# Gated cross attention: where the next quad's attention scores stand among TensorE's products

## The chip, the cores and the metric

The kernel runs on one core of one Trainium2 chip. The metric is device time in microseconds for one execution, the median over several runs. The profile comes from one profiled execution on that core; its span is the time from the first to the last instruction.

## The reference

For each of 8 batches, x has 1024 rows of 1024 numbers and the memory has 64 rows of 512. Everything is float32.

```python
memory_proj = einsum('bme,de->bmd', memory, W_mem)
scores = einsum('bnd,bmd->bnm', hidden_states, memory_proj) / sqrt(D)
attn = softmax(scores, axis=-1)
memory_context = einsum('bnm,bmd->bnd', attn, memory_proj)
gate_input = concatenate([hidden_states, memory_context], axis=-1)
gate = sigmoid(einsum('bnf,df->bnd', gate_input, W_gate) + b_gate)
fused = hidden_states + gate * memory_context
out = rmsnorm(fused, norm_w)
```

Here hidden_states is x, and rmsnorm divides a row by the root of its mean square and multiplies by norm_w (all ones).

## The kernel before, in words

**Quads.** The rows of x are taken in 16 quads of 512 rows, two to a batch (QPB is 2). For each quad the large product is x times the upper half of W_gate, 512 by 1024 times 1024 by 1024. The lower half of W_gate is folded into the memory beforehand (mgd), so that the context's part of the gate needs only the 64 attention weights of a row.

**Products.** The large product is done by a scheme of Strassen's kind with seven products in place of eight, at two levels. The outer level has seven outer products, in the order 1, 6, 7, 5, 4, 2, 3 (ORDER). Each is made of seven inner products named A, B, C, D, A again, E and F. One inner product is two matmuls of 128 by 128 by 256. So a quad has 49 inner products, and the kernel counts them as slots: SLOTS is 49, and slot 0 is the first inner product of outer product 1. Outer product number i in the order has the slots 7i to 7i + 6.

**Operands.** The left operands are quarters of the quad, transposed: A[q, r, h], in tiles a11, a12, a21 and a22, written by transpose_x on VectorE (eight transposes a quad). From them outer_s makes S1 to S4 on VectorE; S3 overwrites a21. For each outer product, inner_s makes four more sums on GpSimd, in tiles l2 (two buffers, two parts of two sums). Results are gathered in the gate tiles O by sums on VectorE (fin) and GpSimd (pre); every inner product has one of five PSUM banks, which come free when VectorE or ScalarE has read them.

**Attention.** scores(q) makes the scores of a quad, transposed: 16 matmuls of 128 rows by 64 columns of weights, in which two matmuls at a time go to the two column halves of the array (tile psT). ScalarE copies them to sT, TensorE transposes them back (sc), softmax_a and softmax_b run on VectorE and ScalarE, and TensorE transposes the weights (pa). In the outer products 5, 4, 2 and 3 a context block stands between the second A and E: 16 matmuls of 64 rows by 128 columns, two at a time on the two row halves, half of which make the context (pc) and half of which add the context's part of the gate to the banks A, F, E and D.

**After the products.** sigmoid on ScalarE, times the context on VectorE (gated), plus the rows of x by an accumulating DMA that GpSimd issues (residual), the mean square on ScalarE (square), and norm on VectorE, in two halves a row block, with the store behind the second.

**What sets the order.** The order on each engine is the order of the program text (pin keeps it). plan(q) writes down what else happens at which slot: at(slot, f) runs f before the inner product of that slot, and mid((q, o), f) runs f right behind the context block of outer product o, before VectorE's first two sums of that block. An engine runs its instructions in that order and waits for each one's inputs and buffers.

The names that matter below:

- scores (lines 295 to 309): 16 matmuls and ScalarE's copy.
- outer_s (254 to 266): S3 and S4 among others.
- transpose_x (239 to 252).
- add_bias (371 and 372): an accumulating DMA on GpSimd's queue, once a batch; load_mg (366 to 369) loads what it adds to.
- norm (603 to 622), placed by the list named when (799 to 809) at the end of outer products 4 and 3. Outer product 4 ends at slot 35, so its offsets count from there.
- plan (530 to 563) and product (676 to 683).

Of the kernel before, what the change touches and what calls it, by code (L numbers as in the profile page):

```python
# [20 lines left out]
def tile_gated_cross_attention_rmsnorm(  # L21
# [46 lines left out]
    QPB = N // QT  # L68
# [31 lines left out]
    def t4k(pool, shape, tag, name):  # L100
        return pool.tile(shape, F32, tag=tag, name=name)
# [33 lines left out]
    for k in range(KD):  # L135
        t = t4k(*((gpool, [P, D], "gate") if k < 7 else (apool, [P, D], "s4")), f"w2_{k}")
# [383 lines left out]
    def at(slot, fn, *args):  # L520
        due.setdefault(slot, []).append(lambda: fn(*args))

    def mid(key, fn, *args):
        beside.setdefault(key, []).append(lambda: fn(*args))
# [5 lines left out]
    def plan(q):  # L530
        t0 = SLOTS * q
        nxt = q + 1 < NQ
        order = [o for o, _ in ORDER]
        for i, o in enumerate(order):
            for part, t in ((0, 1), (1, 5)):
                if i + 1 < len(order):
                    at(t0 + 7 * i + t, inner_s, q, order[i + 1], part)
                elif nxt:
                    at(t0 + 7 * i + t, inner_s, q + 1, order[0], part)
        at(t0 + 7, scores, q)  # L540
        at(t0 + 7, outer_s, q, 3)
        at(t0 + 7, outer_s, q, 4)
        at(t0 + 9, transpose_scores, q)
        at(t0 + 10, softmax_a, q)
        at(t0 + 13, softmax_b, q)
        at(t0 + 18, transpose_attn, q)
        at(t0 + 21, attn_difference, q)
        if not nxt:
            at(t0 + 5, load_last)
            return  # L550
        at(t0 + 2, load_xq, q + 1)
        for t in (2, 3):
            mid((q, 5), transpose_x, q + 1, t, 0)
            mid((q, 2), transpose_x, q + 1, t, 1)
        for i, t, half in ((36, 0, 0), (38, 1, 0), (43, 0, 1), (45, 1, 1)):
            at(t0 + i, transpose_x, q + 1, t, half)
        mid((q, 3), outer_s, q + 1, 1)
        mid((q, 3), outer_s, q + 1, 2)
        if (q + 1) % QPB == 0:
            at(t0 + 10, load_mp, (q + 1) // QPB)  # L560
            at(t0 + 49, load_mg, (q + 1) // QPB)
        if q % QPB == 0:
            at(t0 + 8, add_bias, q // QPB)

    for o in (2, 3):
        w1_place(o)
# [97 lines left out]
    def sqrt_table():  # L664

        t = t4k(small, [P, 1], "warm", "warm")
        pin(nc.scalar.activation(t, eps_sb, AF.Sqrt))

    def outer_product(q, o, ext):
# [113 lines left out]
        if o in (4, 3) and q + 1 == NQ:  # L783
            c, d = 2 * ext[0], 2 * ext[0] + 1
            if o == 3:
                sqrt_table()
            first = (4, 5) if o == 4 else (3, 3)
            at(slot + first[0], last_root, d)
            at(slot + first[1], last_root, c)
            for i, t in enumerate((d, c)):  # L790
                for h_ in range(2):
                    at(slot + first[1] + 1 + 2 * i + h_, last_norm, t, h_)
        elif o in (4, 3):

            row = ext[0]
            c, d = 2 * row, 2 * row + 1
            for t in (d, c):
                at(slot + 5, residual, q, t)
            if row == 0:
                when = (17, 18, 23, 29, None, None)  # L800
            else:
                when = (17, 18, 23, 25, 26, 28)
            at(slot + when[0], square, q, c)
            at(slot + when[1], square, q, d)
            for w_, (t, h_) in zip(when[2:], ((c, 0), (c, 1), (d, 0), (d, 1))):
                if w_ is None:
                    mid((q + 1, 4), norm, q, t, h_)
                else:
                    at(slot + w_, norm, q, t, h_)
# [3 lines left out]
    for q in range(NQ):  # L813
        plan(q)
        for o, ext in ORDER:
            outer_product(q, o, ext)
# [29 lines left out]
```

## Time and profile before

| what | value |
|---|---|
| median of 3 runs | 980.77 us (980.74 to 981.12) |
| span of the profiled execution | 979.4 us |
| granted TensorE clock | 0.996 of full |
| TensorE (PE) busy | 964.8 us, 99% |
| VectorE (DVE) busy | 820.4 us, 84% |
| GpSimd (POOL) busy | 730.5 us, 75% |
| ScalarE (ACT) busy | 324.9 us, 33% |
| scores of one quad to scores of the next | 55.05 us |

The profile is a page with the busy time of each engine, the chain of work that ended last, and groups of instructions. A trace behind it answers for stretches of the span: what ran when, who waited for whom, and the chain in order of time. PE is the matmuls, PEld the loading of weights into the array, which can run beside a matmul. A float32 matmul leaves two records in the trace, so an inner product of two matmuls shows as x4 and the scores of a quad as x32. Ends of matmul records are modelled; starts are the firmer number. Busy time of an engine that nobody waits for costs nothing.

### The profile page before, as it was taken

How to read it: one execution, taken by the hardware profiler on the slowest of the kernel's cores; microseconds unless marked ns; L12 is line 12 of the kernel's file. 1: busy time of each engine (PE TensorE's matmuls, PEld its weight loads, DVE VectorE, ACT ScalarE, POOL GpSimd, SP SyncE). 2: the span in 40 equal slices, each digit the busy share in tenths (PEclk: the TensorE clock that was granted, in tenths of full speed). 3: DMA queues.
4: the chain of work that ended last, by engine and by line, in shares of the span. 5: the costliest groups of instructions: out<-in, count | busy, mean ns of one | idle time of the engine just before them, and what ended most of it. 6: DMA issues, size and time to landing. Idle time of an engine off the chain costs nothing.

```text
span 979.4 us, 14277 instructions
## 1 busy us (share of the span) xinstructions
PE 964.8 (99%) x4938; PEld 769.8 (79%) x4938; DVE 820.4 (84%) x1487; ACT 324.9 (33%) x602; POOL 730.5 (75%) x881
## 2 busy tenths in 40 slices
PE   9999999999999999999999999999999999999995
PEld 6546888888887888888887888888887888888873
DVE  3888788979797988979797988979797988979787
ACT  1100234151433334151433334151433334151434
POOL 3366877878787877878787877878787877878772
PEclk9999999999999999999999999999999999999998
DMA  9865264482918374482918374482818364482612
GB/s 372 258 153 145 39 120 107 103 188 62 186 65 165 108 141 106 102 190 65 183 65 164 111 138 105 107 184 66 182 65 168 110 136 104 108 184 68 169 65 86
DMA packets 71255, 128.32 MB, mean 131 GB/s; under 512 B 12432, under 2 KB 49296, under 8 KB 70928
## 3 DMA queue, kind: packets, MB, share of 16 engines
q1 hardware_dynamic: 61760, 93.34, 35.3%
q0 software_dynamic: 9280, 33.56, 18.5%
q8 instruction: 39, 0.64, 0.3%
q10 hardware_dynamic: 144, 0.52, 0.2%
q14 instruction: 32, 0.26, 0.1%
HBM read 87.56 MB, written 39.85 MB: 130 GB/s over the span
## 4 chain that ended last, share of the span: by engine, by line
PE 96%; DVE 2%; DMA 1%; issue 0%; ACT 0%; POOL 0%; DVEq 0%; ACTq 0%
PE kA L92 20%; PE pc L92 12%; PE kE L92 11%; PE kF L92 10%; PE kD L92 10%; PE kC L92 10%; PE kB L92 10%; PE psT L92 6%; PE pg L92 5%; PE pm L92 3%; DVE gate L95 1%; DMA memq<-in_mem 1%; DVE gate L660 0%; PE pa L342 0%; PE sc L316 0%
## 5 line engine op out<-in xcount | busy, mean ns | idle before, releaser
L95 POOL TENSOR_TENSOR gate<-gate,u 128x256 f32<-128x256 f32 x336 | 270.4, 835 | 115.7 <-DVE u L95 110.1
L582 ACT ACTIVATE gate<-gate 128x512 f32<-128x512 f32 x128 | 79.0, 629 | 400.1 <-DVE gate L95 400.1
L95 POOL TENSOR_TENSOR l<-a 128x256 f32<-128x256 f32 x128 | 128.9, 1007 | 60.4 <-DVE a L95 55.8
L248 DVE STREAM_TRANSPOSE a<-xq 128x512 f32<-128x512 f32 x128 | 137.9, 1098 | 4.0 <-DMA xq<-in_x 4.0
L92 PE MATMUL pc<-mg,attnT 64*128 64x256 f32 x512 | 127.4, 389 | 0.0
L611 DVE SCALAR_TENSOR_TENSOR gate<-gate,ss,nw_sb 128x512 f32<-128x512 f32 x120 | 126.0, 1060 | 1.1
L92 PE MATMUL kD<-it,l 128*128 128x256 f32 x448 | 115.0, 379 | 0.0
L92 PE MATMUL kB<-it,l 128*128 128x256 f32 x448 | 115.0, 379 | 0.0
L92 PEld LDWEIGHTS pc<-mg,attnT 64*128 64x128 f32 x512 | 90.6, 186 | 29.7 <-issue 21.2
L92 PE MATMUL kA<-w,a 128*128 128x256 f32 x384 | 98.7, 379 | 0.4 <-ACT u L726 0.4
L92 PEld LDWEIGHTS kD<-it,l 128*128 128x128 f32 x448 | 85.1, 190 | 11.6
L92 PEld LDWEIGHTS kB<-it,l 128*128 128x128 f32 x448 | 85.1, 190 | 11.6
L95 DVE TENSOR_TENSOR gate<-gate,pc 128x512 f32<-128x512 f32 x128 | 87.0, 680 | 5.8 <-ACT gate L582 5.8
L95 POOL TENSOR_TENSOR l<-s 128x256 f32<-128x256 f32 x96 | 75.7, 789 | 10.8 <-PE kF L92 10.7
L92 PEld LDWEIGHTS kA<-w,a 128*128 128x128 f32 x384 | 71.6, 190 | 10.2 <-ACT u L726 0.8
L726 ACT COPY u<-kA 128x256 f32<-128x256 f32 x112 | 40.5, 362 | 102.1 <-PE kA L92 99.9
L92 PE MATMUL kE<-it,a 128*128 128x256 f32 x256 | 69.0, 392 | 0.0
L95 DVE TENSOR_TENSOR u<-u,kB 128x256 f32<-128x256 f32 x112 | 45.5, 406 | 28.1 <-PE kB L92 24.9
L92 PE MATMUL kA<-t,s 128*128 128x256 f32 x256 | 67.4, 386 | 0.0
L92 PE MATMUL kC<-w,l 128*128 128x256 f32 x256 | 65.7, 379 | 0.0
L92 PE MATMUL kF<-w,l 128*128 128x256 f32 x256 | 65.7, 379 | 0.0
L596 ACT ACTIVATE junk<-gate 128x1024 f32<-128x1024 f32 x60 | 63.5, 1059 | 2.1 <-DMA gate<-in_x 1.2
(123 smaller groups left out, 1996.6 us busy)
## 6 DMA issues: line engine op xcount, KB each, us to landing
xq<-in_x SPq DMA_DIRECT2D x64, 512.0 KB, 9.6
gate<-in_x POOLq DMA_DIRECT2D x60, 512.0 KB, 7.8
out<-gate SPq DMA_DIRECT2D x60, 512.0 KB, 2.6
w<-in_w_gate_t SPq DMA_DIRECT2D x8, 512.0 KB, 11.0
w<-in_w_gate_t SPq DMA_DIRECT2D x2, 2048.0 KB, 15.6
mg<-mgd SPq DMA_DIRECT2D x16, 256.0 KB, 4.0
mpd<-mpT SPq DMA_DIRECT2D x4, 512.0 KB, 3.8
mgd<-mpq SPq DMA_DIRECT2D x16, 128.0 KB, 2.6
```

Of the source, the lines that this page charges most:

```text
L92: pin(nc.tensor.matmul(o, lhsT, rhs, start=start, stop=stop, skip_group_check=True))
L95: pin(eng.tensor_tensor(o, a, b, op))
L248: nc.vector.transpose(A[key][:, :, r * P : (r + 1) * P], chunks(xq[q][:, 4 * t : 4 * t + 4, :], KD)[:, half * KH : (half + 1) * KH],)
L582: pin(nc.scalar.activation(g, g, AF.Sigmoid))
L596: nc.scalar.activation(junk, O[q, t], AF.Square, accum_out=ss[:, t % 2 : t % 2 + 1])
L611: nc.vector.scalar_tensor_tensor(g[:, cols], g[:, cols], rstd[:, t % 2 : t % 2 + 1], nw_sb[:, cols], ALU.mult, ALU.mult,)
L726: pin(nc.scalar.copy(p1, kb["A"]))
```

## The change

The change moves instructions in time and alters none of them: every engine has as many as before. It is meant to bring two kinds of small matmul next to each other on TensorE.

- The scores of quad q + 1 are computed in quad q, right behind the context block of outer product 3 and before its E. Only quad 0 keeps its scores at slot 7.
- S3 moves from slot 7 to slot 6 and S4 from slot 7 to slot 20 (quads 1 to 15), since neither has to stand behind the scores any longer.
- The last two transposes of the next quad move from slots 43 and 45 to slots 42 and 43, so that the scores find them done.
- The norm halves of the fourth row block, which stood at slots 12 and 14 of the next quad (35 + 26 and 35 + 28, less 49), move to slots 15 and 18.
- The bias is added at slot 4 in place of slot 8, except in quad 0.

```diff
-        at(t0 + 7, scores, q)
-        at(t0 + 7, outer_s, q, 3)
-        at(t0 + 7, outer_s, q, 4)
+        if q == 0:
+            at(t0 + 7, scores, q)
+        at(t0 + (6 if q else 7), outer_s, q, 3)
+        at(t0 + (20 if q else 7), outer_s, q, 4)
         at(t0 + 9, transpose_scores, q)
...
-        for i, t, half in ((36, 0, 0), (38, 1, 0), (43, 0, 1), (45, 1, 1)):
+        for i, t, half in ((36, 0, 0), (38, 1, 0), (42, 0, 1), (43, 1, 1)):
             at(t0 + i, transpose_x, q + 1, t, half)
+        mid((q, 3), scores, q + 1)
         mid((q, 3), outer_s, q + 1, 1)
         mid((q, 3), outer_s, q + 1, 2)
...
         if q % QPB == 0:
-            at(t0 + 8, add_bias, q // QPB)
+            at(t0 + (4 if q else 8), add_bias, q // QPB)
...
             if row == 0:
                 when = (17, 18, 23, 29, None, None)
             else:
-                when = (17, 18, 23, 25, 26, 28)
+                when = (17, 18, 23, 25, 29, 32)
```

## The prediction

> **What bounds the kernel now.** I read the page first, then what TensorE waited for, then one steady stretch of the span, then the chain of waits in that stretch, the weight loads and the VectorE timeline.
>
> The page: busy time, and the chain that ended last by engine.
>
> ```profile
> PE 964.8 (99%) x4938; PEld 769.8 (79%) x4938; DVE 820.4 (84%) x1487; ACT 324.9 (33%) x602; POOL 730.5 (75%) x881
> ...
> PE 96%; DVE 2%; DMA 1%; issue 0%; ACT 0%; POOL 0%; DVEq 0%; ACTq 0%
> ```
>
> The waits of TensorE in the whole span (total us, times, longest), its costliest row, and then one quad, from its scores (psT) to the scores of the next: length, busy time of each engine with counts, clock, DMA.
>
> ```profile
> PE kA L92 <- ACT u L726: 1.6, 3, 1.1
> ```
>
> ```profile
> 531.16:586.21 55.05, 55.05 (x299) 45.23 (x300) 47.31 (x88) 19.83 (x36) 44.13 (x54) 1.00 0.62 135
> ```
>
> TensorE is never idle inside a quad, its clock is full, and no engine holds it up: DVE works 47.31 of 55.05 us, GpSimd 44.13. So only fewer or cheaper TensorE microseconds can shorten the quad. That all matmuls stay the same does not settle it, because the chain shows that equal matmuls do not cost the same (start, us, what):
>
> ```profile
> 530.30 0.86 PE kF L92 x4
> 531.16 3.60 PE psT L92 x32
> 534.77 1.06 PE kA L92 x4
> 535.83 0.86 PE kB L92 x4
> ...
> 575.45 0.86 PE kA L92 x4
> 576.31 0.41 PE pc L92
> ...
> 578.24 1.06 PE kE L92 x4
> 579.30 0.86 PE kF L92 x4
> ```
>
> A product (four records of 128 rows by 128 columns) takes 0.86 us, 0.216 a record. The first product after the scores takes 1.06, and so does the first after the context block (pc): 0.20 us more. The scores themselves are 32 records, two at a time on the two column halves, so 16 x 0.216 = 3.45; they take 3.60, 0.15 more. The context block is 16 records on the two row halves, 8 x 0.216 = 1.73, and takes 578.24 - 576.31 = 1.93, 0.20 more. The weight loads say where this goes:
>
> ```profile
> 199.64 0.84 PEld L92 LDWEIGHTS kF<-w,l 128*128 128x128 f32 x4
> 200.81 3.22 PEld L92 LDWEIGHTS psT<-a,mpb 128*64 128x64 f32 x32 [0.33 <-issue]
> ```
>
> In kF the loads run one record ahead of their matmul (the first load at 199.64, its matmul at 199.86 in the TensorE timeline). At the first score the load starts only at 200.81, with its matmul, after 0.33 us in which the loads stood still and waited for nothing that the profile shows.
>
> So one quad has ten changes of array shape: into and out of four context blocks, into and out of the scores. The price list is 0.20 us into a context block, 0.20 back to full products, 0.15 into the scores. Check: 49 products x 0.864 = 42.34; four context blocks x 1.73 = 6.91; scores 3.45; the transposes of scores and weights 2 x 0.22 = 0.44; changes 5 x 0.20 + 4 x 0.20 + 0.15 = 1.95. Sum 55.09, measured 55.05.
>
> [...] 0.15 to 0.20 us at every change, none inside a block where only the tile changes. [...] here 64 columns take 137 ns and 128 take 190, which fits the entry into the scores being 0.05 cheaper. [...]
>
> **The change, part by part.**
>
> Scores of quads 1 to 15 go from in front of outer product 6 to behind the context block of outer product 3 of the quad before, still in front of that product's E. Before, per quad: full to rows, rows to full (product 3), full to columns, columns to full (scores): 0.20 + 0.20 + 0.15 + 0.20 = 0.75. After: full to rows 0.20, rows to columns, columns to full 0.20. Rows to columns is nowhere in the trace. Bounds: nothing (the load could run ahead), or two full changes, 0.35, as if the array went through its whole shape. I take 0.15, the measured entry into the scores, since what is waited for (end of the last matmul, then one load of 64 columns that nothing hides) is the same from either side. Then 0.55 after, 0.20 us saved a quad, 15 quads: 3.0 us. Quad 0 keeps its scores at slot 7, and quad 15 has no next, so its tail is as before.
>
> New waits of the moved scores. They read all four transposed tiles of the next quad. The last two transposes go from slots 43 and 45 to 42 and 43. The VectorE timeline there:
>
> ```profile
> 572.11 0.42 DVE L95 TENSOR_TENSOR gate<-gate,kF 128x256 f32<-128x256 f32 x1 [0.44 <-PE kF L92]
> ...
> 574.07 0.38 DVE L95 TENSOR_TENSOR u<-u,kB 128x256 f32<-128x256 f32 x1
> ...
> 576.33 0.39 DVE L95 TENSOR_TENSOR u<-u,kD 128x256 f32<-128x256 f32 x1
> ```
>
> At 572.11 VectorE is ahead of TensorE, so no backlog comes in. Behind that sum stand, after the change, transpose (1.11), gate product (0.69), transpose (1.11): with the overlap of neighbours seen in this timeline about 2.6 us, so both are done near 575.2. The scores would start at 578.2 and touch these tiles half way, 1.73 us later: 4.7 us to spare. Queued behind the two transposes is the sum with kB, 1.1 us later, done near 575.5. For it waits the bank that the context block reuses as kF, written from 576.78 on in the TensorE timeline: 1.2 us to spare. The sum with kD ends as before, near 576.7, since the same work stands in front of it; its bank is written again at 577.64. On ScalarE the copy of the scores now waits in front of two sigmoids that need product E, which comes behind the scores anyway: nothing.
>
> S3 at slot 6 and S4 at slot 20, 1.23 and 1.22 us on VectorE. Before, S3 waits for the scores (1.47 idle) and VectorE is idle 1.35 more at 536.80. After, S3 falls between two sums of product 1, with those idle times as cover; GpSimd's halves for product 7 start when S3 is there, about at the start of product 6 as before (it stood idle 3.7 us for it). S4 costs 1.2 us near slot 20, where VectorE had small idle times (0.23, 0.26, 0.26) and is next waiting for TensorE at 549.33. Two norm halves (1.06 each, slots 12 and 14 to 15 and 18) leave the crowded stretch in front of it. From 536.80 to 549.33 there are 12.5 us; the work there was 11.5 and becomes 12.7, of which 0.2 can spill; each bank concerned has over 1.5 us. Hidden by TensorE's products: nothing.
>
> GpSimd's bias DMA (0.83 us of issue, three times in all) from slot 8 to 4: its data's load waits only for the last context block, now some 5 us ahead of slot 0, so it does not hold the queue behind it (two residual DMAs, two halves for product 6). Nothing.
>
> What GpSimd loses is the 3.6 us of scores between the halves for product 6 and their use at slot 8. These were done at 530.7 for a use at 535.8; after, counted from the start of product 1, two of them start as TensorE leaves product 3 and the four with the two DMA issues need about 5.2 us (rows of 0.7 to 1.05 and 0.89), against 6.9 us to slot 8. Close, but free.
>
> Sum: 15 x 0.20 = 3.0 us off 980.77: 977.8.
>
> **The rivals.**
>
> Rows to columns is free. For it: inside a shape loads run ahead. Against: every change seen in this trace stops the loads 0.33 us. Then 0.35 a quad, 15 x 0.35 = 5.2 us: 975.6.
>
> Rows to columns costs both full changes, 0.35. Nothing in the trace speaks for it but that it has no such change. Then no gain: 980.8, the same.
>
> Slower: a bank or a GpSimd half comes late every quad, where the scores at slot 7 had let both engines catch up (DVE idle 2.8, GpSimd 3.7 there). The tightest margins above are 0.9 to 1.7 us. If one of them is overrun so that TensorE stands 0.5 us a quad, the change is 15 x (0.5 - 0.2) = 4.5 us: 985.3. Against it: at 572.11 and 563.07 VectorE waits for TensorE, so backlogs do not carry over, and the moved scores give the same 3.6 us of slack at slot 47.
>
> **How the numbers follow.** My forecast has 0.74, free change 0.10, full price 0.09, stall 0.07. Forecast and free change are faster by over 0.2% (2.0 us): faster 0.84; same 0.09; slower 0.07. The range takes the free change in (975.6, so 975.4), and above the forecast it goes to 979.0, where 1.2 of the 3.0 us are lost to stalls in a few quads; what is left out is no gain and slower, 0.16.
>
> **What would show it.** In the chain of the changed kernel: context block 1.93, psT 3.60 directly behind it, then kE 1.06, and in front of product 6 a kA of 0.86; scores to scores 54.85 us in place of 55.05; no wait of TensorE in a steady quad. psT of 3.45 would show the free change; psT of 3.8 the full price. A wait of PE for DVE, POOL or ACT repeated in each quad, most likely at kB or kC of product 6 or at kF or kD in the context block of product 3, would prove the forecast wrong.

## The result and the profile after

| | before | after |
|---|---|---|
| median of 6 runs each, us | 980.94 (980.74 to 981.18) | 990.66 (989.37 to 991.94) |
| ratio | 1 | 1.0099 (95%: 1.0086 to 1.0112) |
| span of the profiled execution, us | 979.4 | 987.5 |

The change costs 9.7 us where a gain of 3.0 was forecast. The page of the changed kernel, busy time and the chain by engine:

```profile
PE 965.9 (98%) x4938; PEld 770.4 (78%) x4938; DVE 821.4 (83%) x1487; ACT 326.9 (33%) x602; POOL 737.2 (75%) x881
...
PE 80%; DMA 9%; DVE 3%; ACT 3%; POOL 2%; issue 2%; DVEq 0%; POOLq 0%; ACTq 0%
```

TensorE's busy time is up by 1.1 us only, and no engine is busy for a larger share of the span than before. What is new is in the chain: 9% of it are now DMA, 1% before. Most of what the span grew by is idle time behind transfers. First, though, the part that was forecast, in the chain of waits of the changed kernel around the moved scores (start, us, what):

```profile
246.67 0.41 PE pc L92
...
248.59 3.60 PE psT L92 x32
252.20 1.06 PE kE L92 x4
253.26 0.86 PE kF L92 x4
```

The context block takes 248.59 - 246.67 = 1.92, the scores directly behind it 3.60, the product behind them 1.06: the three numbers of the forecast. So going from row halves to column halves costs the 0.15 us that was taken for it, and 0.20 us a quad are saved. The stretches of two quads (quads are counted from 0), scores to scores, with busy time by engine, show that something else eats them (length, then PE, PEld, DVE, ACT, POOL, clock, DMA):

```profile
192.20:248.52 56.32, 55.25 (x298) 45.23 (x296) 47.14 (x89) 19.93 (x36) 44.53 (x55) 1.00 0.58 127
248.52:303.57 55.05, 55.05 (x299) 45.30 (x297) 47.70 (x89) 19.84 (x36) 43.85 (x54) 1.00 0.56 120
```

Forecast was 54.85. The odd quads (second of a batch) take 55.03 to 55.05, the first of them 54.94. The even quads (first of a batch, 2 to 14) take 56.33, 55.96, 56.02, 56.75, 57.39, 55.40 and 56.22, at the full clock and with TensorE idle. Over 54.85 the even quads have 10.1 us, the odd ones 1.2; 11.3 less the 3.0 saved is 8.3, and the span grew by 8.1. Which waits these are, the list of waits says (us in total, times, longest; L598 is the square, with junk as its output, and L728 the copy u):

```profile
ACT junk L598 <- DMA gate<-in_x: 24.7, 7, 4.7
...
PE kA L92 <- ACT u L728: 8.6, 9, 1.9
```

```profile
PEld kC L92 <- POOL l L95: 4.8, 15, 0.7
```

Before, kA waited 1.6 us for u, three times, at the end of the span (from 944 us on). The other 7.0 us are new: in six of the seven even quads (all but quad 12) the second A of outer product 5 waits for u, ScalarE's copy that frees its bank. The chain through one of them (start, us, what):

```profile
199.90 1.05 POOL gate L588
200.95 14.01 DMA gate<-in_x
...
216.16 1.15 ACT junk L598 x2
...
217.33 1.28 ACT L603
...
220.47 0.38 ACT u L728
...
220.90 1.13 PE kA L92 x4
```

Read from below: TensorE's kA at 220.90 starts when u is done at 220.85. That copy stood in ScalarE's queue behind two squares, a table load and the copies of the attention weights, and the first square waited for a residual DMA that GpSimd issued at 200.95 and that landed 14.01 us later. The same stretch of ScalarE's timeline in both kernels, after and then before:

```profile
211.00 0.37 ACT L728 COPY u<-kA 128x256 f32<-128x256 f32 x1 [2.47 <-PE kA L92]
214.98 1.06 ACT L598 ACTIVATE junk<-gate 128x1024 f32<-128x1024 f32 x1 [3.61 <-DMA gate<-in_x]
...
220.47 0.37 ACT L728 COPY u<-kA 128x256 f32<-128x256 f32 x1
```

```profile
211.85 0.37 ACT L726 COPY u<-kA 128x256 f32<-128x256 f32 x1 [2.47 <-PE kA L92]
212.12 1.06 ACT L596 ACTIVATE junk<-gate 128x1024 f32<-128x1024 f32 x1
...
218.17 0.37 ACT L726 COPY u<-kA 128x256 f32<-128x256 f32 x1 [0.58 <-PE kA L92]
```

The issue of that transfer and the second A of product 5 in the kernel before, in the timelines of GpSimd and TensorE, and then the same A in the changed kernel:

```profile
198.09 0.88 POOL L586 DMA_DIRECT2D gate<-in_x  x1 [0.19 <-issue]
```

```profile
220.50 1.03 PE L92 MATMUL kA<-t,s 128*128 128x256 f32 x4
```

```profile
220.90 1.13 PE L92 MATMUL kA<-t,s 128*128 128x256 f32 x4 [1.07 <-ACT u L728]
```

Before, ScalarE came to the square at 212.12, just as the transfer landed (issued 198.09, landed 212.04), and later was 0.58 us early at u. That copy was done at 218.54 for an A that started at 220.50, so 1.96 + 0.58 = 2.54 us of delay could be absorbed. After, ScalarE is free at 211.37 and waits 3.61 us; 3.61 - 2.54 = 1.07, which is what kA waits. The transfer takes as long as before, 14.0 us; it is the distance from its issue to the square that shrank, from 14.0 to 10.4 us, which is the length of the scores. They used to stand between the two and now stand in front of the issue. That the two transfers take the same time is the sum of two effects, as the first experiment shows.

The second new wait is smaller: kC waits for GpSimd. In the odd quads, and in quad 12, it is kC of product 5. Timelines of TensorE, VectorE and GpSimd of the changed kernel in quad 3:

```profile
273.39 1.03 PE L92 MATMUL kB<-it,l 128*128 128x256 f32 x4
274.35 1.13 PE L92 MATMUL kC<-t,l 128*128 128x256 f32 x4
275.32 1.03 PE L92 MATMUL kD<-it,l 128*128 128x256 f32 x4
```

```profile
272.31 1.40 DVE L95 TENSOR_TENSOR s<-a,s 128x1024 f32<-128x1024 f32 x1
```

```profile
272.59 1.71 POOL L95 TENSOR_TENSOR l<-s 128x256 f32<-128x256 f32 x1
```

The starts of B, C and D are 0.96 and 0.97 us apart in place of 0.86, so 0.2 us are lost a quad. GpSimd's sum for C took 1.71 us, where the same sum for product 5 takes 0.72 and 0.73 in the last two kernels below, without S4 beside it; here it ran beside S4, which the change put here. In the other even quads it is kC of product 4, behind the stall: VectorE's sum waits for the late copy u, and GpSimd's sums for product 4 stand behind sums that need VectorE's (in quad 2 GpSimd waits 1.86 us for it).

### The profile page after: what moved, and what is told of

Same layout as the page of the kernel before. It is cut to its first block, busy times and chain, and to the rows that moved or that the text cites. A ratio compares the mean times of both kernels' runs of the same rounds, so it can differ in the third digit from the quotient of the medians.

```text
span 987.5 us, 14301 instructions
## 1 busy us (share of the span) xinstructions
PE 965.9 (98%) x4938; PEld 770.4 (78%) x4938; DVE 821.4 (83%) x1487; ACT 326.9 (33%) x602; POOL 737.2 (75%) x881
## 4 chain that ended last, share of the span: by engine, by line
PE 80%; DMA 9%; DVE 3%; ACT 3%; POOL 2%; issue 2%; DVEq 0%; POOLq 0%; ACTq 0%
PE kA L92 15%; PE pc L92 12%; PE kE L92 9%; DMA gate<-in_x 9%; PE kF L92 8%; PE kC L92 8%; PE kD L92 7%; PE kB L92 7%; PE psT L92 6%; PE pg L92 5%; PE pm L92 3%; DVE gate L95 1%; POOL l L95 1%; ACT junk L598 1%; ACT L603 1%
## 5 line engine op out<-in xcount | busy, mean ns | idle before, releaser
L95 POOL TENSOR_TENSOR gate<-gate,u 128x256 f32<-128x256 f32 x336 | 291.9, 897 | 120.5 <-DVE u L95 118.6
L613 DVE SCALAR_TENSOR_TENSOR gate<-gate,ss,nw_sb 128x512 f32<-128x512 f32 x120 | 123.0, 1035 | 1.1
L95 POOL TENSOR_TENSOR l<-a 128x256 f32<-128x256 f32 x128 | 103.1, 805 | 25.1 <-PE kA L92 19.3
L95 POOL TENSOR_TENSOR l<-s 128x256 f32<-128x256 f32 x96 | 88.2, 919 | 40.2 <-PE kF L92 40.2
L95 DVE TENSOR_TENSOR gate<-gate,kE 128x256 f32<-128x256 f32 x112 | 45.5, 419 | 42.9 <-PE kE L92 41.1
L92 PEld LDWEIGHTS kA<-w,a 128*128 128x128 f32 x384 | 71.8, 190 | 10.1 <-ACT u L728 0.8
L728 ACT COPY u<-kA 128x256 f32<-128x256 f32 x112 | 40.5, 361 | 109.7 <-PE kA L92 107.5
L598 ACT ACTIVATE junk<-gate 128x1024 f32<-128x1024 f32 x60 | 63.5, 1058 | 25.6 <-DMA gate<-in_x 24.7
## 6 DMA issues: line engine op xcount, KB each, us to landing
xq<-in_x SPq DMA_DIRECT2D x64, 512.0 KB, 10.1
```

The costliest lines, as they stand in the source:

```text
L92: pin(nc.tensor.matmul(o, lhsT, rhs, start=start, stop=stop, skip_group_check=True))
L95: pin(eng.tensor_tensor(o, a, b, op))
L598: nc.scalar.activation(junk, O[q, t], AF.Square, accum_out=ss[:, t % 2 : t % 2 + 1])
L613: nc.vector.scalar_tensor_tensor(g[:, cols], g[:, cols], rstd[:, t % 2 : t % 2 + 1], nw_sb[:, cols], ALU.mult, ALU.mult,)
L728: pin(nc.scalar.copy(p1, kb["A"]))
```

## The experiments

The theory after this: two losses, one from the residual DMAs through ScalarE's queue, in even quads, and one from S4 at slot 20. A first rival to it: the moved scores themselves are at fault, since GpSimd and VectorE lost their 3.6 us to catch up. Edits are against the changed kernel unless said otherwise; the kernel before, run on the same chips, took 980.8 to 980.9 us.

**The bias back at slot 8.** In the changed kernel the bias DMA stands in front of the two residual DMAs in GpSimd's queue.

```diff
-            at(t0 + (4 if q else 8), add_bias, q // QPB)
+            at(t0 + 8, add_bias, q // QPB)
```

> The changed kernel with the bias DMA back at slot 8 (behind the two residual DMAs in GpSimd's software queue), everything else as changed. Theory A (the bias DMA stands in front of the residual DMAs in the same queue in the first quad of each batch, the squares on ScalarE wait for the residuals, ScalarE copies the first half of product 5 late, TensorE's second A of product 5 waits): the waits of kA for ScalarE in the even quads go (about 7 stalls, 8.6 us with their dearer first records), ScalarE's wait for the residuals falls from 24.7 us to under 6, and the time falls to about 981.5. What stays is 0.2 us a quad at kC of product 5. Rival B (the 3.6 us that the scores took between residual and squares are missing, whatever the bias does): the stalls stay at half or more, time 985 or over. Rival C (S4 at slot 20 is the cause): no change, 989 to 991.

Measured 984.52 us (983.79 to 985.94), ratio 1.0038 (1.0025 to 1.0051): 6.1 us better than the change. From the list of waits of this kernel, the row of the residuals:

```profile
ACT junk L598 <- DMA gate<-in_x: 14.0, 7, 2.5
```

The second residual of quad 2 now lands 12.00 us after its issue in place of 14.01; over the seven even quads the means are 12.4 and 13.8. ScalarE's wait falls from 24.7 to 14.0 us, and the new waits for u are all but gone (kA 1.7, as before). So the bias in front makes the second residual 1.4 us later on average, 2.0 in quad 2. In the kernel before, with the bias behind it too, the mean was 13.7: with the scores moved the transfer itself is 1.3 us quicker, for a reason that was not taken apart, and the bias in front takes that back. The expectation had under 6 us of ScalarE's wait and about 981.5. The 14.0 us that stay are 2.0 us a batch, which fit into the 2.54 us of room and hardly stop TensorE. What is left of TensorE's loss is kC of product 5 or 4, and one quad of 57.50 us in which a norm half took 3.90 us; more of that below.

**S4 back at slot 7, and both together.**

```diff
-        at(t0 + (20 if q else 7), outer_s, q, 4)
+        at(t0 + 7, outer_s, q, 4)
```

> The changed kernel with S4 back at slot 7, the bias still at slot 4. Theory A with its second part (S4 on VectorE at slot 20 runs beside GpSimd's sum for kC of product 5 and makes it 1.7 us long in place of 0.7, so that kC waits 0.2 us in nearly every quad): kC of product 5 starts on time, 13 to 14 fewer waits, 2.6 us; the stalls at A of product 5 in the even quads stay. Time about 987. Rival C (S4 is behind the stalls too): about 978 to 981. Rival D (S4 at slot 7 without the scores' 3.6 us in front of it delays VectorE): kB or kC of product 6 wait, time not below 989.

> The changed kernel with both back: bias at slot 8, S4 at slot 7. Theory A in both parts: only the saving of the moved scores is left, 0.2 us in 15 quads, period 54.85 us, time about 978.0, faster than before by 0.3%. If it is not below 980.5, a third cause (missing slack of the scores, rival B, or the moved norm halves) is at work.

S4 alone: 986.01 us, ratio 1.0050 (1.0035 to 1.0065). The wait at kC of product 5 is gone. The stalls for u stay, but at half the size (4.2 us in place of 8.6), so that most of what this run gains comes from them: its residuals land sooner (13.58 us after the issue in place of 15.07 in quad 10), and why was not taken apart. Both: 980.30 us, ratio 0.9995 (0.9987 to 1.0004), with no new stall at u and none at that kC: the two edits account for both losses. But of the saving of 3.0 only 0.5 comes out, where 978 was expected: S4 at slot 7 has its own price. In the timelines of TensorE and VectorE of the kernel with both:

```profile
320.22 1.03 PE L92 MATMUL kA<-w,a 128*128 128x256 f32 x4
321.13 1.13 PE L92 MATMUL kB<-it,l 128*128 128x256 f32 x4
322.10 1.03 PE L92 MATMUL kC<-w,l 128*128 128x256 f32 x4
```

```profile
315.10 1.71 DVE L95 TENSOR_TENSOR s<-a,s 128x1024 f32<-128x1024 f32 x1
...
320.67 0.41 DVE L95 TENSOR_TENSOR gate<-gate,kD 128x256 f32<-128x256 f32 x1
```

Here kB of product 7 needs the bank of kD of product 6, which VectorE reads only at 320.67. Starts are 0.91 and 0.97 apart: 0.16 us lost, and quads take 55.00 to 55.01. S4 took 1.71 us here (1.22 in the kernel before), with GpSimd's sums beside it.

**The scores alone.** The kernel before, with only the scores moved.

```diff
-        at(t0 + 7, scores, q)
+        if q == 0:
+            at(t0 + 7, scores, q)
...
+        mid((q, 3), scores, q + 1)
```

> The kernel before with only the scores of quads 1 to 15 moved behind the context block of product 3: S3 and S4 at slot 7, transposes at 43 and 45, norm halves at 12 and 14, bias at 8. Theory A: the same saving as with bias and S4 put back, about 978, if VectorE catches up by slot 21 with 2.4 us of S3 and S4 at slot 7 and no pause in front; up to 980 if some sums come late. Rival B (the scores' own time was the slack that the residual needed): stalls at A of product 5 also here, 985 or over.

Measured 1023.09 us, ratio 1.0433 (1.0415 to 1.0450): the expectation missed by over 40 us. Even quads take 60.3 to 60.5 us, odd ones 55.6. The VectorE, GpSimd and TensorE timelines of one even quad:

```profile
207.94 0.75 DVE L613 SCALAR_TENSOR_TENSOR gate<-gate,ss,nw_sb 128x512 f32<-128x512 f32 x1
...
210.07 4.68 DVE L613 SCALAR_TENSOR_TENSOR gate<-gate,ss,nw_sb 128x512 f32<-128x512 f32 x1
```

```profile
209.23 0.82 POOL L372 DMA_DIRECT2D mg<-in_b_gate  x1
```

```profile
210.87 1.03 PE L92 MATMUL kA<-w,a 128*128 128x256 f32 x4
215.46 2.08 PE L92 MATMUL kB<-it,l 128*128 128x256 f32 x4 [3.56 <-DVE gate L95]
217.33 1.72 PE L92 MATMUL kC<-w,l 128*128 128x256 f32 x4
218.89 1.03 PE L92 MATMUL kD<-it,l 128*128 128x256 f32 x4
```

A norm half that takes 0.75 us at 207.94 takes 4.68 when it starts 0.84 us behind the issue of the bias DMA. The sums behind it come late, kB of product 7 stands for 3.56 us, and then kB and kC take 3.43 us together (215.46 to 218.89) in place of 1.73. That is 3.56 + 1.70 = 5.3 us a batch, seven times, 37 of the 45 us over the forecast. The starts of quad 3, against those of a quad of 54.85, give the 0.8 us of the odd ones: 0.28 at kB of product 7, 0.12 in front of the transposes of the weights and 0.37 at kC of product 5. No wait for u is new (kA 1.7). So the rival is right in part: the moved scores alone do not bring the stall at u, but without them VectorE and GpSimd come late elsewhere, and the other edits of the change do real work. The bias at slot 4 keeps it away from that norm half.

**S4 at slot 5, with the bias at 8 and at 6.** At slot 5 S4 runs ahead of the crowded stretch of slots 6 to 9.

```diff
-        at(t0 + (20 if q else 7), outer_s, q, 4)
+        at(t0 + (5 if q else 7), outer_s, q, 4)
...
-            at(t0 + (4 if q else 8), add_bias, q // QPB)
+            at(t0 + 8, add_bias, q // QPB)
```

> The changed kernel with the bias DMA at slot 8 and S4 at slot 5, where VectorE stood idle for 1 us in front of product E of outer product 1 and GpSimd's sums there have 2 us to spare; S3 stays at 6. Theory A (bias in front of the residuals, S4 beside GpSimd's sum for kC of product 5, and S4 at 7 too late for the bank of kB of product 7): all three losses gone, period 54.85 us, time about 978.0, 0.3% under before. If kB of product 7 still waits as with S4 at slot 7, S4's place was not its cause and the time is 980. If S4 right behind the residual DMAs is drawn out by GpSimd's work for them, kB of product 6 waits and the time is over 981.

Measured 1016.22 us, ratio 1.0362 (1.0339 to 1.0385), again far off. The odd quads take 54.85, the forecast, so slot 5 costs TensorE nothing, though S4 takes 2.4 us there beside two of GpSimd's sums, in place of 1.22. In seven even quads the norm half is held again:

```profile
208.70 4.68 DVE L613 SCALAR_TENSOR_TENSOR gate<-gate,ss,nw_sb 128x512 f32<-128x512 f32 x1
```

It starts 0.84 us behind the issue (207.86), as in the run above. The next run has the bias at `(6 if q else 8)` and is otherwise the same:

> As the one before, but the bias at slot 6: behind the two residual DMAs in GpSimd's software queue, in the 1.3 us in which GpSimd waits for product 7's operand. Theory A says that only the order against the residuals matters: 978.0, the same as with slot 8. If a two-input VectorE operation (S3, S4) that starts about 0.7 to 1.6 us after the issue of a software DMA is held until 5.5 us after it, as the norm halves were in the kernel with the scores alone moved, S3 takes 4 to 5 us in 7 quads and the time is 985 to 1005.

Measured 978.49 us, ratio 0.9975 (0.9965 to 0.9984). No norm half is held, nor S3, which starts 1.7 us behind the issue and takes 1.21; eleven of the 14 quads from quad 1 on take 54.85, and 55.27, 55.17 and 55.05 are left, all even (in quad 4 the time goes at the second A of product 5 and at kC of product 4). Two slots of one DMA's place are worth 38 us.

**The bias alone.** The kernel before, with only the bias at `(4 if q else 8)`.

> The kernel before with the bias alone moved to slot 4, in front of the residuals; the scores stay at slot 7. Theory A in its full form (the bias makes the second residual land 2 to 2.5 us later, but the scores' 3.6 us between residual and squares hide it; only both changes together hurt): ScalarE waits 1 to 3 us a batch for the residuals, TensorE does not wait for it, time 980.9, the same. Rival (the bias in front is enough): stalls at A of product 5, 986 or over.

Measured 982.55 us, ratio 1.0018 (1.0010 to 1.0026), 1.7 us over the expected 980.9. ScalarE waits 14.3 us for residuals (1.2 in the kernel before), as long as with the bias back at slot 8 and the scores moved (14.0). The second residual of quad 2 lands 15.60 us after its issue in place of 13.96 (means of the even quads 15.0 and 13.7). Before the end of the span TensorE waits for u once, 0.29 us in quad 2. So either edit alone makes ScalarE wait 2.0 us a batch, which is nearly absorbed; with both it waits 3.5 us, which is more than the room.

**The squares later.** If the stall goes through ScalarE's queue, it must vanish when the squares stand behind the copy u, with the DMAs left as the change has them. The first two numbers place the squares.

```diff
-                when = (17, 18, 23, 29, None, None)
+                when = (22, 23, 26, 29, None, None)
```

> The changed kernel, bias at slot 4 and S4 at 20 as changed, but the two squares of the first row half move from slots 17 and 18 to 22 and 23, and the first norm half behind them from 23 to 26. If the stall goes through ScalarE's queue (squares wait for the residuals, behind them the four copies of the attention weights and the first copy of product 5), ScalarE no longer waits at these copies, A of product 5 starts on time in all quads, and 7 to 9 us come back: about 981 to 983, with the 0.2 us a quad at kC of product 5 left. If the late residuals hurt by another way, the time stays at 987 or over.

Measured 980.49 us, ratio 0.9996 (0.9987 to 1.0004), 10.2 us better than the change, where 7 to 9 were expected. No wait for residuals is in the list, kA waits 2.0 us for u (three times, at the end of the span), and even quads take 54.85 to 55.1. The odd ones still have 55.03 to 55.05: the loss at kC of product 5 is untouched. The bias still stands in front of the residuals here (14.59 us to landing in quad 2), so the lateness of the transfers by itself does not stop TensorE; the stall came through what stood behind the squares on ScalarE.

**All three mended, and the norms put back.** S4 at slot 5, bias at slot 6, squares at 22 and 23:

> The changed kernel with S4 at slot 5, the bias at slot 6 and the squares of the first row half at slots 22 and 23 (their first norm half at 26): each of the three losses removed in its own way. By the theory every quad from 2 to 15 takes 54.85 us, ScalarE never waits for a residual with something of TensorE's behind it, and the time is 977.8, the forecast of the bare saving, 0.3% under before and some 0.5 us under the version with the squares at 17 and 18, with less spread. If it is over 978.5, the late squares cost something of their own (the norm half at 26 behind product E of outer product 5).

Measured 978.06 us (977.94 to 978.28), ratio 0.9970 (0.9959 to 0.9981): 0.3% faster than the kernel before, and faster than the change. The stretch from scores to scores and the waits of TensorE for u:

```profile
192.48:247.33 54.85, 54.85 (x299) 45.31 (x297) 47.70 (x89) 19.84 (x36) 44.31 (x55) 1.00 0.59 130
```

```profile
PE kA L92 <- ACT u L728: 1.6, 3, 1.1
```

Every quad from quad 1 on takes 54.85 but one, 54.95. The same with the two norm halves at their old places:

```diff
-                when = (17, 18, 23, 25, 29, 32)
+                when = (17, 18, 23, 25, 26, 28)
```

> As the one before, with the two norm halves of the fourth row block back at slots 12 and 14. Theory: with S4 out of the way VectorE enters product 6 without backlog, so the halves at 12 and 14 do no harm and the time is the same, 977.8 to 978.2. Rival: the half at slot 12 stands in front of the sums that free the bank of kB of product 7, kB waits 0.1 to 0.2 us a quad, 979.5 to 980.5.

Measured 983.61 us, ratio 1.0027 (1.0017 to 1.0037): a miss, and not at the place that the rival named. TensorE's timeline, and its longest new wait:

```profile
217.84 1.03 PE L92 MATMUL kB<-it,l 128*128 128x256 f32 x4
218.96 1.13 PE L92 MATMUL kC<-t,l 128*128 128x256 f32 x4
219.92 1.03 PE L92 MATMUL kD<-it,l 128*128 128x256 f32 x4
```

```profile
PEld kC L92 <- POOL l L95: 7.0, 15, 0.5
```

B to C is 1.12 and C to D 0.96 in place of 0.86 each: 0.36 us a quad, some 5 us in 14 quads, of 5.5 us between the two kernels. It is kC of product 5 again, late from GpSimd, and the timelines of VectorE and GpSimd say why. First this kernel, then the one with the norm halves at 15 and 18, whose quad started 0.49 us earlier:

```profile
215.56 0.42 DVE L95 TENSOR_TENSOR u<-u,kC 128x256 f32<-128x256 f32 x1
```

```profile
218.17 0.73 POOL L95 TENSOR_TENSOR l<-s 128x256 f32<-128x256 f32 x1
```

```profile
213.94 0.42 DVE L95 TENSOR_TENSOR u<-u,kC 128x256 f32<-128x256 f32 x1
```

```profile
217.01 0.72 POOL L95 TENSOR_TENSOR l<-s 128x256 f32<-128x256 f32 x1
```

One norm half more (1.24 us) stands on VectorE in front of the sum with kC of product 7, which so comes 1.13 us later in the quad. Three sums of GpSimd start 0.14 us behind its end in both kernels, and the sum for kC of product 5 stands behind them. With the scores moved, the norm halves may not stay where they were.

## Why the prediction was wrong

**What bounds it, and the price of a change of shape: right.** TensorE bounds a steady quad, and the saving is 0.20 us a quad: 55.05 became 54.85 wherever nothing is late, and the kernel with the three mends takes 978.06 where 977.8 was forecast. Rows to columns is neither free nor at full price: the scores take 3.60 us in place of 3.45, as they do behind full products, and in both places the weight loads stand still 0.33 us and then start with their matmul (248.52 in the changed kernel, 200.81 before). That the load waits for the end of the last matmul was my estimate; the rows do not name what it waits for.

**Transposes and banks of the moved scores: right.** No wait of the moved scores, of E or of F for VectorE appears; the scores follow the context block at once.

**The failed step: "GpSimd's bias DMA (0.83 us of issue, three times in all) from slot 8 to 4 ... it does not hold the queue behind it ... Nothing."** The count was wrong too, with seven batches behind the first. The issue does not hold GpSimd's instructions for long (it starts at 199.35 and those of the residuals follow from 199.90 on), but with that transfer in front of them the second of the two residuals lands later (14.01 us after its issue against 12.00 with the bias behind, in quad 2; 13.8 against 12.4 in the mean), and it has a reader with a date: ScalarE's square.

**The same step's other half: "What GpSimd loses is the 3.6 us of scores between the halves for product 6 and their use at slot 8."** I charged the lost 3.6 us to GpSimd's sums only. For GpSimd's halves of product 6 that was right: no wait for them appears. But the scores also stood between the residuals' issue and the squares, 14.0 us before and 10.4 after. In the profile of before this was to be seen: the transfer landed at 212.04 and its square began at 212.12, a margin of 0.08 us, behind which stood a copy that frees a bank of TensorE. The prediction lists margins of 0.9 us and more, and of ScalarE's work only the copy of the scores; the squares and the copies u are in none of its terms. The room of 2.54 us takes the 2.0 us of either edit alone, and not the 3.61 of both. Cost: 7.0 us of TensorE's waits in six quads.

**The second failed step: "S4 costs 1.2 us near slot 20 ... Hidden by TensorE's products: nothing."** VectorE itself does have the room (busy for 47.70 of the 55.05 us of quad 3). What was left out is GpSimd's sum beside S4: it takes 1.71 us there, in place of the 0.72 and 0.73 without S4 beside it, and was needed within that time. S4 took longer too, 1.40 us in quad 3 against 1.22 in the kernel before. Side by side both take longer, as these durations show; by what means, no run shows. Cost at that kC: about 0.2 us in each odd quad.

**The rival that came true** is the stall that was given 0.07, but little of it is right beyond the sign: it was to come in every quad, at product 6 or in the context block of product 3, and to give 985.3. The larger loss is in every second quad, at product 5, through a DMA and ScalarE's queue; only the smaller one is a late GpSimd half, as the rival had it. 990.66 is also 1.2 us above the profiled run's own 989.42; runs of this kernel spread over 2.6 us, before over 0.4. That the transfers' landing times make the spread is a guess; it was not tried.

## What to carry to other kernels

When instructions move on the engine that is the bound, every distance that spanned them shrinks: list each transfer whose issue and first reader stood on either side, and compare the time left with the time it took to land, not with the busy share of the engine that reads it. ScalarE, 33% busy, stopped TensorE here for 7.0 us, because what waited in its queue stood ahead of a copy that frees a bank; placing the late reader behind that copy cured it without touching the transfer (990.66 us became 980.49). When a small DMA or a VectorE sum is moved, ask what it stands next to: here the slower neighbours cost more than it did itself (a norm half of 4.68 us behind an issue of 0.82, a GpSimd sum of 1.71 in place of 0.73 us beside S4).

## What the runs showed of the hardware

**A norm half held behind a DMA issue.** In three of the kernels a norm half on VectorE (SCALAR_TENSOR_TENSOR) that started 0.72 to 1.63 us behind the issue of the bias DMA ended 5.52 us behind that issue, in all 15 cases: seven with the scores alone moved, seven with S4 at slot 5 and the bias at 8, and one with the bias at slot 8 (869.60 + 3.90 = 873.50, issue at 867.97). Halves that started between 0.5 us ahead of it and 0.55 behind it, or from 2.03 to 4.4 us behind it, took 0.75 to 1.24. The hold outlasts any one of GpSimd's instructions: with the scores alone moved, GpSimd's sums ran on beside the half of 4.68 us, the four from 211.86 on in 0.96 to 1.07 us each. Nor is every operation of VectorE held behind every issue: S4 at slot 5 started 1.00 to 1.11 us behind the issue of a residual in four kernels and took 2.29 to 2.40 us, in all 60 cases. What is shown, for norm halves behind the bias DMA, is the dependence on the distance to the issue; the mechanism stays open.

**Slow records after idle time.** When TensorE had stood for 3.56 us (kB of product 7 above), the records that followed ran at 426 ns in place of 216, for about eight records, in all seven cases. The stretch behind the stall, in the kernel with the scores alone moved, shows the granted clock (last but two) at 0.54:

```profile
215.40:219.00 3.60, 3.54 (x9) 2.89 (x10) 3.26 (x9) 2.13 (x4) 0.00 (x0) 0.54 0.36 146
```

A stall of 3.56 us so cost 5.3. With S4 at slot 5 and the bias at 8, where TensorE stood some 3.1 us, six of the seven stalls show such records as well; behind the stalls of up to 1.9 us in the changed kernel no record ran at 426. How long TensorE must stand for it, the runs do not show more closely than that.
